# A four-layer graph network on one core: ScalarE's and VectorE's instruction orders given by the program instead of the scheduler

## The chip, the core and the metric

The kernel runs on one core of a Trainium2 chip, in one launch. The metric is the device time of that launch in microseconds (us). Five engines work side by side, each on its own list of instructions: TensorE (PE: matrix products), VectorE (DVE), ScalarE (ACT: here the exponentials), GpSimd (POOL) and SyncE (SP: it issues the transfers). An instruction waits until the work that it needs on other engines has been reported done.

## The reference

16 graphs of 1024 nodes with 128 features share one adjacency matrix (about 1 entry in 64 is set). Three layers of masked attention with 8 heads follow each other, and then a last layer in which an edge's weight depends on a sum of two node values. Cut to what matters:

```python
# layers 0, 1, 2, for every graph
Q, K, V = h @ Wq, h @ Wk, h @ Wv                        # 8 heads of 16
scores = einsum('bnhd,bmhd->bhnm', Q, K) / sqrt(16)
scores = where(adj == 0, -inf, scores)
attn = softmax(scores, axis=-1)
x = layer_norm(h + einsum('bhnm,bmhd->bnhd', attn, V) @ Wo + bo)
x = layer_norm(x + relu(x @ W1 + b1) @ W2 + b2)
# layer 3
h = x @ W;  e = leaky_relu((h @ a_src)[:, None] + (h @ a_dst)[None, :])
out = layer_norm(softmax(where(adj == 0, -inf, e)) @ h + x)
```

## The kernel before

One graph in one attention layer is a block; there are 48 of them. A block is cut into 32 steps: two groups of four heads, two halves of the queries (512 each), eight tiles `kt` of 128 keys. A step makes the scores of four heads in two pairs. Each pair fills a slot of PSUM of 128 x 1024 f32, and there are three slots, taken in turn. The masking is done in one of two ways: ScalarE takes the exponential straight from PSUM and GpSimd then multiplies by a mask of 0 and 1 (first pair, in five of eight steps), or VectorE adds a mask of 0 and a large negative number and ScalarE takes the exponential of the result (all other pairs). Whoever reads PSUM (ScalarE or VectorE) frees the slot. The numbers behind `# L` are the lines under which the profile lists an instruction.

```python
AHEAD = 4                      # a step's product with V comes four steps later
BOTH_ON_DVE = (2, 5, 7)        # kt in which VectorE masks both pairs

def slot(dtype=F32):
    return psum.tile([P, N], dtype, tag="s", name="s", bufs=3)
def bank():                    # for everything but the scores
    return psum.tile([P, 512], F32, tag="t", name="t", bufs=1)
def e_tile():
    return work.tile([P, J, 512], F32, tag="e", name="e", bufs=6)

def score_step(step):
    m, g, qh, kt = step
    e = e_tile()
    q0 = qh * 512
    for pp in range(2):
        q, k = state["Wq", g, pp], state["Wk", g, pp]
        ps = slot()
        for r in range(2):
            nc.tensor.matmul(ps[:, r * 512:(r + 1) * 512], ...)                # L395
        ev = e[:, 2 * pp:2 * pp + 2, :]
        psv = ps.rearrange("p (r q) -> p r q", q=512)
        on_pool = pp == 0 and kt not in BOTH_ON_DVE
        m = (mask01 if on_pool else mask_add)[...]
        if on_pool:
            nc.scalar.activation(ev, psv, AF.Exp, scale=HD ** -0.5)            # L402
            nc.gpsimd.tensor_mul(ev, ev, m)                                    # L403
        else:
            nc.vector.tensor_add(ev, psv, m)                                   # L405
            nc.scalar.activation(ev, ev, AF.Exp, scale=HD ** -0.5)             # L406
    return e

def av_step(step, e, acc, first, last):      # e @ V, and the sums, into the one bank acc
    ... nc.tensor.matmul(acc[...], v_bufs[...], e[:, j, :], start=first, stop=last)   # L412
def finish(g, qh, acc):                      # after eight steps
    ... with soon():
        nc.vector.transpose(tt, acc)                                           # L423
    nc.vector.reciprocal(rec, tt[:, :, HD])                                    # L425
    nc.gpsimd.tensor_mul(state["A"][...], tt[:, :, :HD], rec[...])             # L426
```

Everything else (projections of the next block, output product and feed-forward of the block before, the last layer of finished graphs) is cut into tasks. At most one task is taken up in a step, behind the step's score and V products. Its products go into the one bank `t`, which ScalarE or VectorE must empty before the next task's products can start. `soon()` raises an instruction's priority with the scheduler.

```python
# transposes (L260) -> ScalarE copy xT, x1T (L263, L265)
# split: x @ Wq, x @ Wk (L271) -> ScalarE hi (L359), VectorE lo = t - hi (L360)
# v (L271, 32 small products) -> ScalarE copy (L366)
# gather: VectorE transposes A into aT (L439), range check of the sums (L327)
# out_proj, ffn2 (L271; 32 and 64 small products) -> VectorE
def add_and_stats(n):
    def out(ts, ps):
        with soon():
            nc.vector.tensor_add(n[0][:, ts, :], v3(ps), n[0][:, ts, :])       # L303
        stats(n, ts)               # four bn_stats (L296), four bn_aggr (L298)
# then GpSimd normalises (L311 to L315)
# ffn1 (L271) -> ScalarE relu hT (L468)
# last layer: nodes (L529), edges (L569 -> VectorE L572),
#             aggregate (L581, 32 products -> VectorE L584, L587, stats)
```

The loop over all steps runs with TensorE's order fixed by the program; the orders of ScalarE, VectorE and GpSimd are chosen when the kernel is built, by a scheduler that works with priorities and its own estimate of durations. Once built, every engine's order is fixed.

```python
with tc.manual_schedule(engines={mybir.EngineType.PE}):
    for m, (b, l) in enumerate(blocks):
        ...
            e = score_step(step)
            waiting.append((step, e, n + AHEAD))
            av_due(n)              # the V products that are due, and finish()
            piece()                # one task
            n += 1
    for n in range(n, n + 2 * AHEAD):
        now[0] = n
        av_due(n)
        piece()
```

Of the kernel before, what the change touches and what calls it, by code (L numbers as in the profile page):

```python
# [14 lines left out]
AF = mybir.ActivationFunctionType  # L15
# [5 lines left out]
HD = 16  # L21
# [10 lines left out]
BOTH_ON_DVE = (2, 5, 7)  # L32
# [74 lines left out]
def fast_path(ctx: ExitStack, tc: tile.TileContext, a: dict, out: bass.AP, flag):  # L107
    nc = tc.nc
# [12 lines left out]
    def slot(dtype=F32):  # L121

        return psum.tile([P, N], dtype, tag="s", name="s", bufs=3)
# [9 lines left out]
    def e_tile():  # L133
        return work.tile([P, J, 512], F32, tag="e", name="e", bufs=6)
# [12 lines left out]
    def fetch(b):  # L147
        def run():
            state["x", b] = load_x(b)
        return run  # L150
# [60 lines left out]
    def other_weights():  # L211
        for l in range(1, L):
            W.append(load_layer(nc, nc.sync, const, a, l, [n for n in LAYER if n not in ("ln1_b", "ln2_b")]))
            norm_weights(nc.sync, l)
            add_bias(nc.sync, "ln2_b", l - 1, "bo", l)
            add_bias(nc.sync, "ln1_b", l, "b2", l)
        nc.sync.dma_start(ln2_b_last, rows_of(a[f"L{L - 1}_gnn_ln2_b"]))
        for n in LAST:
            src = a[f"L3_gnn_{n}"]
            if n == "W":  # L220
                t = w_nodes[:, :D]
                nc.sync.dma_start(t, src)
            elif n in ("a_src", "a_dst"):
                t = const.tile([P, 1], F32, name=n)
                nc.sync.dma_start(t, src.rearrange("(p o) -> p o", o=1))
            else:
                t = const.tile([P, D], F32, name=n)
                nc.sync.dma_start(t, rows_of(src))
            wl[n] = t

    def last_weights():
        a2 = const.tile([P, 2], F32)
        nc.vector.tensor_copy(a2[:, 0:1], wl["a_src"])
        nc.vector.tensor_copy(a2[:, 1:2], wl["a_dst"])
        ps = bank()
        nc.tensor.transpose(ps[:, :P], w_nodes[:, :D], identf)
        w3t = work.tile([P, P], F32, tag="row", name="w3t", bufs=2)
        nc.vector.tensor_copy(w3t, ps[:, :P])
        ps = bank()
        nc.tensor.matmul(ps[:, :2], w3t, a2, start=True, stop=True)  # L240
        nc.vector.tensor_copy(w_nodes[:, D:], ps[:, :2])
# [131 lines left out]
    def stack(m, g):  # L373

        for n, order in (("Wk", (0, 1, 0, 1)), ("Wq", (0, 0, 1, 1))):
            for pp in range(2):
                t = work.tile([P, N], F32R, tag=n, name=n, bufs=4)
                r0 = (g * J + 2 * pp) * HD
                for i, part in enumerate(order):
                    nc.sync.dma_start(t[i:P:4, :].bitcast(F32), state[n, m][part][r0:r0 + 2 * HD, :].bitcast(F32))  # L380
                state[n, g, pp] = t
# [5 lines left out]
# [8 lines that stand above are left out]
                nc.tensor.matmul(ps[:, r * 512:(r + 1) * 512], k[64 * r:64 * r + 64, kt * P:(kt + 1) * P],  # L395
                                 q[64 * r:64 * r + 64, q0:q0 + 512], start=True, stop=True)
# [3 lines that stand above are left out]
            m = (mask01 if on_pool else mask_add)[:, kt, q0:q0 + 512][:, None, :].to_broadcast([P, 2, 512])  # L400
            if on_pool:
                nc.scalar.activation(ev, psv, AF.Exp, scale=HD ** -0.5)  # L402
                nc.gpsimd.tensor_mul(ev, ev, m)  # L403
            else:
                nc.vector.tensor_add(ev, psv, m)  # L405
                nc.scalar.activation(ev, ev, AF.Exp, scale=HD ** -0.5)  # L406
        return e

    def av_step(step, e, acc, first, last):
        m, g, qh, kt = step  # L410
        for j in range(J):
            nc.tensor.matmul(acc[j * SLOT:j * SLOT + HD + 1, :], v_bufs[m % 2][:, kt, 2 * j + g, :], e[:, j, :],  # L412
                             start=first, stop=last)
# [204 lines left out]
    def put(tasks, mark, chain=None, first=False):  # L618

        if chain is None:  # L620
            chain = {"due": now[0], "queue": deque()}
            chains.insert(0 if first else len(chains), chain)
        for n, task in enumerate(tasks):
            chain["queue"].append(task + (mark if n == len(tasks) - 1 else None,))
        return chain
# [21 lines left out]
    def need(mark):  # L647
        while mark not in done:
            first = next(c for c in chains if any(q[3] == mark for q in c["queue"]))
            assert take(first) or any(take(c) for c in list(chains) if c is not first)  # L650
# [17 lines left out]
    def av_due(n):  # L668

        for item in [w for w in waiting if w[2] <= n]:  # L670
            step, e, _ = item
            half = step[:3]
            if half not in accs:
                if accs:
                    continue
                accs[half] = sums
                left[half] = NT
            waiting.remove(item)
            left[half] -= 1
            av_step(step, e, accs[half], left[half] == NT - 1, left[half] == 0)  # L680
            if left[half]:
                continue
            m, g, qh = half
            b, l = blocks[m]
            while g == 0 and qh == 0 and last_attn:
                need(last_attn.pop())
            finish(g, qh, accs.pop(half))()
            if m == len(blocks) - 1:
                if g == G - 1:
                    if qh == 0:  # L690
                        final.append(post_tasks(b, l)[1])
                    put(final[0][qh], ("final", qh), first=True)
                    if qh == 1:
                        put(last_tasks(b), ("last", b), chains[0])
            elif g == G - 1 and qh == 1:
                post = post_tasks(b, l)[0]
                chain = put(post[:1], ("attn", b, l))
                put(post[1:], ("post", b, l), chain)
                last_attn.append(("attn", b, l))
                if l == L - 1:  # L700
                    put(last_tasks(b), ("last", b), chain)

    n = 0
    with tc.manual_schedule(engines={mybir.EngineType.PE}):
        for m, (b, l) in enumerate(blocks):
            order = [(g, qh) for g in range(G) for qh in range(2)]
            if m == len(blocks) - 1:
                order.sort(key=lambda x: x[1])
            for at, (g, qh, kt) in enumerate((g, qh, kt) for g, qh in order for kt in range(NT)):
                now[0] = n  # L710
                if at == 1:
                    stack(m, 1)
                if n == 3:
                    other_weights()
                if n == 40:
                    last_weights()
                if at == 0 and m + 2 < len(blocks) and blocks[m + 2][1] == 0:
                    put([(0, fetch(blocks[m + 2][0]), "+x")], ("fetch", blocks[m + 2][0]))
                if m + 1 < len(blocks):
                    if at == 6:  # L720
                        need(("post",) + (blocks[m + 1][0], blocks[m + 1][1] - 1) if blocks[m + 1][1] else
                             ("fetch", blocks[m + 1][0]))
                        put(proj_tasks(m + 1), ("proj", m + 1), first=True)
                    if at == 19:
                        need(("proj", m + 1))
                        stack(m + 1, 0)
                step = m, g, qh, kt
                e = score_step(step)
                waiting.append((step, e, n + AHEAD))
                av_due(n)  # L730
                piece()
                n += 1
        for n in range(n, n + 2 * AHEAD):
            now[0] = n
            av_due(n)
            piece()
        while chains:
            now[0] += 1
            for chain in list(chains):
                if now[0] >= chain["due"] + chain["queue"][0][0]:  # L740
                    take(chain)
# [236 lines left out]
```

## Time and profile before

| | us |
|---|---|
| time, median of three runs (4254.99 to 4259.61) | 4256.9 |
| span of the profiled run, granted TensorE clock 0.98 | 4253.7 |
| TensorE busy | 3892.9 |
| VectorE, ScalarE, GpSimd busy | 3404.9, 3417.3, 3451.4 |
| one masking on VectorE (L405), 2112 of them | 1.212 |
| one exponential of a masked pair (L406), 2112 | 1.060 |
| one exponential from PSUM (L402), 960 | 1.021 |
| one mask product on GpSimd (L403), 960 | 2.151 |

How to read the profile: an entry such as `ACT e L406` is an engine, the tile that it writes and the line. Busy time is the union of an engine's instructions; matmuls overlap each other, and their ends are modelled. A wait is idle time ahead of an instruction, put down to whoever released it last. "PEld" is TensorE's loading of weights, which runs beside its products. In the chain that ended last, each instruction is followed back to the one that released it, and the shares of engines and lines are shares of the span.

### The profile page before, as it was taken

The numbers are of one execution on the slowest core, as the hardware profiler recorded it, in microseconds if no ns is written. First come the engines' busy times: TensorE is split into PE (matmuls) and PEld (weight loads), VectorE is DVE, ScalarE is ACT, GpSimd is POOL, SyncE is SP. The second block draws the span as 40 slices with busy tenths as digits, with TensorE's granted clock in tenths as the row PEclk, the third lists the DMA queues.
The fourth block names the chain that finished last, engine by engine and source line by source line (L and its number), as shares of the span: only waits on it lengthen the run. The fifth ranks groups of instructions, "written<-read, shape, count | busy, mean of one in ns | idle before, by whom it ended". The sixth has DMA issues, their size and how long they took to land.

```text
span 4253.7 us, 93788 instructions
## 1 busy us (share of the span) xinstructions
PE 3892.9 (92%) x37589; PEld 1575.2 (37%) x37589; DVE 3404.9 (80%) x5324; ACT 3417.3 (80%) x3961; POOL 3451.4 (81%) x3010
## 2 busy tenths in 40 slices
PE   7999999999999999999999899999999999999986
PEld 2333333344443333334444333333344433333435
DVE  6888888877777888887777888887877788888784
ACT  7999999876778898987676898997876789998770
POOL 4788888876779888888777988888877798888785
PEclk9999999999999999999999999999999999999997
DMA  5221222121211221221112212221211212212100
GB/s 147 65 61 50 52 61 61 48 63 44 51 51 48 61 61 44 57 61 51 51 44 59 59 48 55 61 61 41 56 48 49 66 41 61 60 47 55 44 24 17
DMA packets 126235, 232.23 MB, mean 55 GB/s; under 512 B 36704, under 2 KB 75616, under 8 KB 125792
## 3 DMA queue, kind: packets, MB, share of 16 engines
q1 hardware_dynamic: 122896, 225.14, 21.0%
q8 instruction: 299, 4.90, 0.5%
q10 hardware_dynamic: 2896, 1.01, 0.1%
q14 instruction: 144, 1.18, 0.1%
HBM read 15.54 MB, written 8.39 MB: 6 GB/s over the span
## 4 chain that ended last, share of the span: by engine, by line
PE 37%; DVE 26%; ACT 23%; issue 7%; POOL 5%; DMA 1%; SPq 1%; DVEq 0%; ACTq 0%; POOLq 0%
DVE e L405 16%; ACT e L406 13%; PE t L271 11%; PE acc L412 10%; PE s L395 9%; ACT e L402 6%; PE t L581 6%; DVE st L296 2%; POOL e L403 2%; DVE tt L423 1%; DVE e L572 1%; DVE x L303 1%; PE t L260 1%; ACT xT L265 1%; DVE lo L360 1%
## 5 line engine op out<-in xcount | busy, mean ns | idle before, releaser
L405 DVE TENSOR_TENSOR e<-s,mask_add 128x1024 f32<-128x1024 f32 x2112 | 2499.4, 1212 | 441.2 <-PE s L395 351.5
L406 ACT ACTIVATE e<-e 128x1024 f32<-128x1024 f32 x2112 | 2200.2, 1060 | 408.2 <-DVE e L405 392.1
L403 POOL TENSOR_TENSOR e<-e,mask 128x1024 f32<-128x1024 f32 x960 | 2054.0, 2151 | 426.1 <-ACT e L402 410.5
L412 PE MATMUL acc<-e,v 128*17 128x512 f32 x12288 | 1635.4, 604 | 56.5 <-DVE tt L423 29.8
L395 PE MATMUL s<-Wq,Wk 64*128 64x512 f32 x6144 | 1225.7, 462 | 137.9 <-ACT e L402 67.9
L402 ACT ACTIVATE e<-s 128x1024 f32<-128x1024 f32 x960 | 980.4, 1021 | 115.0 <-PE s L395 58.4
L395 PEld LDWEIGHTS s<-Wq,Wk 64*128 64x128 f32 x6144 | 505.8, 185 | 1118.5 <-issue 371.5
L412 PEld LDWEIGHTS acc<-e,v 128*17 128x17 f32 x12288 | 207.2, 95 | 558.2 <-issue 445.6
L315 POOL TENSOR_SCALAR x<-x,mv 128x128 f32<-128x128 f32 x896 | 391.4, 452 | 24.1
L319 POOL TENSOR_TENSOR x<-x,ln_g 128x1024 f32<-128x1024 f32 (+1 forms) x97 | 229.4, 2365 | 107.8 <-PE t L260 101.9
L581 PEld LDWEIGHTS t<-hd,e 128*128 128x128 f32 x2048 | 255.2, 205 | 63.7 <-issue 32.5
L581 PE MATMUL t<-hd,e 128*128 128x129 f32 x2048 | 267.2, 292 | 8.3 <-DVE x L587 3.5
L313 POOL TENSOR_TENSOR mv<-mv,half_neg 128x4 f32<-128x4 f32 x224 | 232.4, 1037 | 14.7
L271 PE MATMUL t<-x1T,W 128*32 128x512 f32 x1536 | 206.2, 609 | 18.0 <-ACT hT L468 8.6
L303 DVE TENSOR_TENSOR x<-t,x 128x512 f32<-128x512 f32 x192 | 131.8, 687 | 100.1 <-PE t L271 99.4
L296 DVE BATCH_NORM_STATS2 st<-x 128x6 f32<-128x128 f32 x896 | 196.7, 279 | 2.8
L271 PEld LDWEIGHTS t<-W,hT 128*32 128x32 f32 x6144 | 172.0, 111 | 70.6 <-issue 32.9
L271 PE MATMUL t<-W,hT 128*32 128x128 f32 x6144 | 187.1, 274 | 9.1 <-DVE x L303 5.2
L260 PE MATMUL t<-identf,x 128*128 128x128 f32 x896 | 151.5, 290 | 34.7 <-ACT xT L265 7.8
L260 PEld LDWEIGHTS t<-identf,x 128*128 128x128 f32 x896 | 95.9, 142 | 229.2 <-issue 48.0
L311 POOL TENSOR_SCALAR mv<-mv 128x4 f32<-128x4 f32 x224 | 53.0, 237 | 145.1 <-DVE mv L298 108.4
L468 ACT ACTIVATE hT<-t,b 128x512 f32<-128x512 f32 x192 | 132.3, 689 | 45.6 <-PE t L271 42.6
(83 smaller groups left out, 2509.7 us busy)
## 6 DMA issues: line engine op xcount, KB each, us to landing
Wk<-hi SPq DMA_DIRECT2D x384, 128.0 KB
Wk<-lo SPq DMA_DIRECT2D x384, 128.0 KB
Wq<-hi SPq DMA_DIRECT2D x384, 128.0 KB
Wq<-lo SPq DMA_DIRECT2D x384, 128.0 KB
x<-in_x_dram SPq DMA_DIRECT2D x16, 512.0 KB
out_dram<-x SPq DMA_DIRECT2D x31, 256.0 KB
ai<-in_adj_dram SPq DMA_DIRECT2D x8, 512.0 KB
g_rows<-parts SPq DMA_DIRECT2D x124, 4.0 KB
```

What stands on the lines that cost most here:

```text
L260: nc.tensor.transpose(ps[:, t * P:(t + 1) * P], src[:, 4 * h + t, :], identf)
L271: nc.tensor.matmul(dst[j:j + SLOT, :], lhsT[:, j:j + SLOT], rhs, start=start, stop=stop)
L296: nc.vector.bn_stats(st[:, t, :], z[:, t, :])
L313: nc.gpsimd.tensor_tensor(v, v, half_neg[:, ts], OP.pow)
L315: nc.gpsimd.tensor_scalar(z[:, t, :], z[:, t, :], mv[:, t, 0:1], mv[:, t, 1:2], op0=OP.add, op1=OP.mult)
L395: nc.tensor.matmul(ps[:, r * 512:(r + 1) * 512], k[64 * r:64 * r + 64, kt * P:(kt + 1) * P], q[64 * r:64 * r + 64, q0:q0 + 512], start=Tru ...
L402: nc.scalar.activation(ev, psv, AF.Exp, scale=HD ** -0.5)
L403: nc.gpsimd.tensor_mul(ev, ev, m)
L405: nc.vector.tensor_add(ev, psv, m)
L406: nc.scalar.activation(ev, ev, AF.Exp, scale=HD ** -0.5)
L412: nc.tensor.matmul(acc[j * SLOT:j * SLOT + HD + 1, :], v_bufs[m % 2][:, kt, 2 * j + g, :], e[:, j, :], start=first, stop=last)
L581: nc.tensor.matmul(ps[:, i * (D + 1):(i + 1) * (D + 1)], e[:, t, i * P:(i + 1) * P], s["hd"][t // 4][:, t % 4, :], start=(t == 0), stop=(t ...
```

## The change

ScalarE's and VectorE's orders in the loop are now given by the program too, as TensorE's was: each engine executes its instructions in the order in which the program writes them. So that ScalarE doesn't stand before a masking that VectorE has only just begun, the exponential of a masked pair isn't written at once but put on a list. `exponentials()` is called at the end of each step's scores and writes those that are due: the second pair's of the step before, and, in the steps in which VectorE masks both pairs, the first pair's of this one. All other work of VectorE in a step (transpose of the sums, a task's subtraction, addition and statistics) comes behind the step's maskings, as it is written there. `soon()` has no effect on these two engines any more. GpSimd's order is still the scheduler's.

```diff
@@ score_step
             else:
                 nc.vector.tensor_add(ev, psv, m)
-                nc.scalar.activation(ev, ev, AF.Exp, scale=HD ** -0.5)
+                masked.append((2 * step_no[0] + pp + (kt not in BOTH_ON_DVE), ev))
+        step_no[0] += 1
+        exponentials()
         return e
+
+    masked, step_no = [], [0]
+
+    def exponentials(n=None):
+
+        while masked and (n is not None or masked[0][0] < 2 * step_no[0] - 1):
+            _, ev = masked.pop(0)
+            nc.scalar.activation(ev, ev, AF.Exp, scale=HD ** -0.5)
@@ the loop over all steps
-    with tc.manual_schedule(engines={mybir.EngineType.PE}):
+    with tc.manual_schedule(engines={mybir.EngineType.PE, mybir.EngineType.Activation, mybir.EngineType.DVE}):
@@ after the last step
+        exponentials(0)
         for n in range(n, n + 2 * AHEAD):
             now[0] = n
             av_due(n)
```

In the changed kernel L406 is L417, and the lines from L412 on are ten or eleven higher (L412 is L422, L423 is L433).

## The prediction

> **What bounds the kernel now.** I read the page first (busy shares and the chain that ended last), then the waits, then the timeline of one block engine by engine. The page shows four engines that are all nearly full, and a chain that goes round TensorE, VectorE and ScalarE:
>
> ```profile
> PE 3892.9 (92%) x37589; PEld 1575.2 (37%) x37589; DVE 3404.9 (80%) x5324; ACT 3417.3 (80%) x3961; POOL 3451.4 (81%) x3010
> ...
> PE 37%; DVE 26%; ACT 23%; issue 7%; POOL 5%; DMA 1%; SPq 1%; DVEq 0%; ACTq 0%; POOLq 0%
> DVE e L405 16%; ACT e L406 13%; PE t L271 11%; PE acc L412 10%; PE s L395 9%; ACT e L402 6%; PE t L581 6%; DVE st L296 2%; POOL e L403 2%; DVE tt L423 1%; DVE e L572 1%; DVE x L303 1%; PE t L260 1%; ACT xT L265 1%; DVE lo L360 1%
> ```
>
> TensorE is the longest, with 4254 - 3893 = 361 us idle. No change to the other engines' orders can bring more than that plus what is hidden in stretched matmuls. The waits (engine, line, whom it waited for: us in total, times, longest) say who holds whom:
>
> ```profile
> ACT e L406 <- DVE e L405: 392.1, 446, 5.3
> DVE e L405 <- PE s L395: 351.5, 442, 7.8
> DVE col L584 <- PE t L581: 175.8, 64, 11.5
> PE s L395 <- ACT e L402: 67.9, 138, 0.9
> PE t L271 <- DVE lo L360: 41.1, 47, 1.5
> PE s L395 <- DVE e L405: 32.8, 58, 1.7
> PE acc L412 <- DVE tt L423: 29.8, 78, 0.7
> ```
>
> ScalarE's largest wait, 392 us, is for VectorE's masking; it is what the change attacks. But TensorE, the bound, loses only 68 us to a late exponential (L402, which frees a score slot), 33 us to late masking, 41 us to `lo` and 30 us to the transpose of the sums. The 392 us are mostly idle time of an engine that isn't the bottleneck.
>
> **One block in detail.** The middle of the run repeats with a period of 77.2 us for a block of 32 steps. The windows view of such a block, and of the stretch without tasks in it (us; then busy of PE, PEld, DVE, ACT, POOL; clock, DMA):
>
> ```profile
> 505.00:582.20 77.20, 72.32 (x722) 25.42 (x720) 65.30 (x97) 70.08 (x79) 67.22 (x56) 1.00 0.23 56
> 564.40:587.30 22.90, 21.25 (x148) 6.10 (x148) 22.40 (x32) 22.18 (x24) 21.50 (x21) 1.00 0.38 93
> ```
>
> From start to start of the scores in TensorE's timeline, an undelayed step costs 1.65 us without a task (572.49 to 574.14), 2.50 with eight L271 (522.51 to 525.01), 2.23 with four transposes, 2.52 with 32 and 3.39 with 64 small matmuls. A block has 14, 8, 4, 4 and 2 of these: 23.1 + 20.0 + 8.9 + 10.1 + 6.8 = 68.9 us. So a block has 77.2 - 68.9 = 8.3 us of delay, of which 77.2 - 72.3 = 4.9 show as idle and 3.4 are hidden in busy.
>
> In the stretch without tasks VectorE is 98% and ScalarE 97% busy: there it is not TensorE that sets the pace. ScalarE back to back takes 2.80 us for three exponentials (581.38 to 584.18):
>
> ```profile
> 581.38 1.02 ACT L402 ACTIVATE e<-s 128x1024 f32<-128x1024 f32 x1
> 582.28 2.01 ACT L406 ACTIVATE e<-e 128x1024 f32<-128x1024 f32 x2
> 584.18 1.03 ACT L402 ACTIVATE e<-s 128x1024 f32<-128x1024 f32 x1
> ```
>
> That is 0.93 each, 1.87 us for a step's two, above TensorE's 1.65.
>
> **What the Trainium skill says.** "PSUM — Partial Sum Buffer", section "Engine vs sequencer instructions": the queues of ScalarE and VectorE are strict first in, first out. So an order chosen by the program is binding: what stands behind a blocked instruction waits. The trace agrees (VectorE stands up to 11.5 us before L584). "ScalarE: Activation LUTs", section "What ACT_TABLE_LOAD costs": 186 ns plus 0.833 ns for each element with immediate scale and bias, and an overlap of about 93 ns back to back; for 1024 elements 1039 and 946 ns. The trace has 1021 to 1060 and 933: agreed. "VectorE: DVE Perf Modes", section "The perf-mode tier table (the rule you actually need)": an addition with a PSUM operand runs at 1x, so no order makes the 1212 ns of L405 shorter; back to back the trace has 7.95 us for seven, 1.14 each.
>
> **The change part by part.** No operation is added or taken away: 960 direct exponentials, 2112 masked ones and 2112 maskings stay. What moves is read from the two built programs' orders.
>
> 1. *ScalarE.* Before, the direct exponential of step n stood behind all masked ones of earlier steps in 683 of 960 cases, one was still owed in 230 and two in 47. After, one is owed in 959 of 960 (in steps with both maskings on VectorE the first one stays in its own step). So the direct exponential, which frees the slot, no longer waits for the last masking. I expect most of the 68 us on TensorE to go where ScalarE isn't itself full. In the ordinary block the timeline has 1.8 us of it, four times; 1.2 happen in the full stretch and stay, so the gain is some 0.6 us a block. The demand there stays: 12 steps without tasks take 562.79 to 585.78 = 23.0 us now, and ScalarE's own work is 12 x 1.87 = 22.4. The step later doesn't reduce that; it only lets ScalarE owe one, never two.
>
> 2. *VectorE, `lo`.* It now follows the step's masking at once, and no other task's work stands between. The 0.9 us that TensorE loses to it in the block (521.50, before a Wo product) goes: 0.9 gained.
>
> 3. *VectorE, statistics ahead of the next masking.* This is a loss. In steps where both maskings are on VectorE (the third, sixth and eighth of every eight), the order before was `x<-t`, first masking, statistics, second masking; the trace shows it:
>
> ```profile
> 562.93 0.69 DVE L303 TENSOR_TENSOR x<-t,x 128x512 f32<-128x512 f32 x1 [0.34 <-PE t L271]
> 563.54 1.22 DVE L405 TENSOR_TENSOR e<-s,mask_add 128x1024 f32<-128x1024 f32 x1
> 564.67 0.86 DVE L296 BATCH_NORM_STATS2 st<-x 128x6 f32<-128x128 f32 x4
> 565.45 0.36 DVE L298 BATCH_NORM_AGGREGATE mv<-st 128x2 f32<-128x6 f32 x4
> 565.73 1.19 DVE L405 TENSOR_TENSOR e<-s,mask_add 128x1024 f32<-128x1024 f32 x1
> ```
>
> After, all statistics (0.86 + 0.36, about 1.1 us with overlap) come ahead of both. The first masking frees the slot that the second score pair of the next step needs, with 0.5 to 1.4 us in hand (a step of 1.65 to 2.5 us, less some 1.15 for the masking itself). It happens twice a block (behind the first Wo product and the second W2 product): I count 1.3 and 1.0 us.
>
> 4. *VectorE, transpose of the sums.* It stood ahead of a masking at times and now always stands behind one (1.2 us) and behind the statistics before it. TensorE has one bank of sums and waits. Idle for it in the block is 0.65 + 0.16 + 0.15 now; I estimate 1.3 more in two of the four places. In blocks with tasks of the last layer both transposes of A also come later, in front of it: 1.4 us, in some 20 blocks, perhaps 20 us in all.
>
> 5. *Last layer's tasks.* Before, L584 stood ahead of maskings that were long ready. After, all of VectorE's work is in TensorE's order, so it waits only for what TensorE hasn't done. Steps with L581 take 6.2 us on average where the undelayed one takes 5.4 (64 steps), and those with L529x4 3.9 against 2.7 (16): 51 + 19 = 70 us, part of it clock (0.69 to 0.72 in some L581 windows). I expect 40 to 60 back.
>
> The sum for a block: -0.6 - 0.9 + 2.3 + 1.3 = +2.1 us, against which stands what I can't count: the 3.4 us hidden in stretched matmuls and 0.9 us of small waits for ScalarE's copies (0.26, 0.24, 0.22, 0.20), all of which come from orders that disagree with TensorE's. If half goes, -2.2: about zero, 0 x 48 blocks. With -50 from part 5, +20 from part 4, and -15 for ScalarE in the last layer's stages: 4257 - 45 = 4212, rounded to 4210 us.
>
> **Rivals.** A: the loop is cut. The 392 us of ScalarE's waiting feed back through the slots (ScalarE late, scores late, masking late), and half of the 8.3 us a block goes: 48 x 4 = 190, with part 5 4257 - 240 = 4017 us. For it: the chain's 29% in L405 and L406. Against it: only 68 us reach TensorE, and the stretch is full on two engines. B: fixed orders lose elasticity. Losses of part 3 and 4 stand, nothing hidden comes back: +2.1 x 48 = +101, less 45: 4310 us. For it: before, ScalarE could owe two in the stretch, and statistics were split. C: the masks on GpSimd (81%) become the bound; its order is still the scheduler's and changes little, 67 of 77 us a block; I give it little.
>
> **Range and chances.** The middle lies between A and B. My count of one block is uncertain by some 2 us either way, 100 us in the whole, so 8 in 10: 4100 to 4320. Under 4172 (2% faster) 0.33, over 4342 0.13, between 0.54.
>
> **What would show it.** Right: ScalarE's wait for L405 well under 200 us; TensorE's wait for L402 under 40; its wait for the transpose (acc) and for L405 up; ordinary block 76 to 78 us. Wrong: a block under 75 us means that the hidden 3.4 us were order and statistics cost nothing (A); over 79 that VectorE's fixed order is the new bound (B).

## The result and the profile after

The changed kernel takes 4360.8 us (median of four runs, 4358.65 to 4362.88) against 4255.9 for the kernel before: a ratio of 1.0245 with a 95% interval of 1.0228 to 1.0263. It is slower, where 4210 had been predicted with a range of 4100 to 4320.

The page gives the busy time of each engine in a span of 4356.9 us:

```profile
PE 3919.2 (90%) x37589; PEld 1579.8 (36%) x37589; DVE 3426.8 (79%) x5324; ACT 3385.4 (78%) x3961; POOL 3454.6 (79%) x3010
```

The instructions are the same in number. TensorE's busy time is 26 us longer and the other three stay within 1%, so most of the 103 us between the two spans is idle time of TensorE. The page's chain of the changed kernel breaks off at its last instructions and shows nothing of the loop. The waits do (engine, line, whom it waited for: us in total, times, longest):

```profile
ACT e L417 <- DVE e L405: 542.1, 355, 5.2
...
DVE lo L360 <- ACT hi L359: 151.7, 146, 2.3
...
PE s L395 <- DVE e L405: 117.3, 146, 2.3
...
PE acc L422 <- DVE tt L433: 73.2, 98, 2.2
...
PE t L271 <- DVE lo L360: 23.2, 42, 1.5
PE s L395 <- ACT e L402: 18.9, 78, 0.6
```

Of TensorE's four waits in the prediction two fell (for L402 from 67.9 to 18.9, for `lo` from 41.1 to 23.2) and two rose by more (for the masking from 32.8 to 117.3, for the transpose of the sums from 29.8 to 73.2). ScalarE's wait for the masking, which the change was to take away, rose from 392 to 542 us. VectorE now stands 152 us before `lo`, which needs ScalarE's `hi`; before, that was 44.7 us.

An ordinary block of the changed kernel, in the windows view (us; then busy of PE, PEld, DVE, ACT, POOL; clock, DMA):

```profile
589.20:667.60 78.40, 72.02 (x724) 25.26 (x720) 65.48 (x97) 69.12 (x79) 67.21 (x56) 1.00 0.21 53
```

The block is 1.2 us longer than the one shown of before, and TensorE's busy time in it is 0.3 us shorter. TensorE's timeline names its larger idle times, in brackets with whom it waited for:

```profile
600.30 0.50 PE L395 MATMUL s<-Wq,Wk 64*128 64x512 f32 x2 [1.10 <-DVE e L405]
...
613.58 1.05 PE L422 MATMUL acc<-e,v 128*17 128x512 f32 x8 [1.28 <-DVE tt L433]
...
651.37 0.50 PE L395 MATMUL s<-Wq,Wk 64*128 64x512 f32 x2 [1.03 <-DVE e L405]
...
654.35 1.05 PE L422 MATMUL acc<-e,v 128*17 128x512 f32 x8 [0.48 <-DVE tt L433]
```

VectorE's timeline at the same place shows what stands ahead of the last two:

```profile
648.33 0.69 DVE L303 TENSOR_TENSOR x<-t,x 128x512 f32<-128x512 f32 x1 [0.34 <-PE t L271]
649.06 0.87 DVE L296 BATCH_NORM_STATS2 st<-x 128x6 f32<-128x128 f32 x4
649.85 0.36 DVE L298 BATCH_NORM_AGGREGATE mv<-st 128x2 f32<-128x6 f32 x4
650.12 3.46 DVE L405 TENSOR_TENSOR e<-s,mask_add 128x1024 f32<-128x1024 f32 x3
653.49 0.71 DVE L433 STREAM_TRANSPOSE tt<-acc 128x512 f32<-128x512 f32 x1
```

The statistics, 1.1 us, pass ahead of three maskings, the first of which TensorE needs for its next slot; and the transpose that frees the bank of sums comes behind all three.

**Where the time went, by blocks.** Taken from start to start of the scores in TensorE's timeline (each block from its fifth step on, when its own V products begin; the first with the four steps ahead of it), the 48 blocks fall in two kinds. In 28 "ordinary" ones (76 to 80 us before) there is little or nothing of the last layer; in the other 20 the last layer's tasks run, or the work ends. Against before, the ordinary blocks of the changed kernel are 40.1 us longer in all and the others 57.9; some 5 us lie outside the blocks. The same count by the kind of task that a step carries, sums in us, for the kernels before and after and the first two experiments below:

| steps of the 28 ordinary blocks | before | after | e1 | e2 |
|---|---|---|---|---|
| no task (386) | 750.5 | 787.8 | 749.0 | 790.5 |
| eight L271 (220) | 613.4 | 578.8 | 563.4 | 617.4 |
| 32 or 64 L271 (164) | 500.0 | 488.5 | 490.1 | 506.2 |
| transposes L260 (117) | 279.0 | 322.9 | 312.2 | 306.0 |
| sum with the rest | 2170.5 | 2210.6 | 2141.5 | 2251.7 |

**The granted clock.** Part of the difference may come by way of TensorE's granted clock and not by waits. Over the span it is 0.980 before and 0.973 after. By the clock records of the two traces it averages 0.970 and 0.960 in the 20 other blocks, 0.998 and 0.996 in the ordinary ones. Block time times what is missing from 1 gives an estimate of the time at full clock that TensorE loses: some 20 us more in the other blocks and 5 in the ordinary ones. It is not the whole loss. In blocks 10 to 15, a stretch of the last layer, both kernels have the same mean clock, and the changed one still takes 14 us more (windows view, before and after):

```profile
815.70:1398.60 582.90, 535.34 (x5041) 235.99 (x5040) 455.22 (x748) 429.36 (x515) 454.56 (x411) 0.96 0.20 51
828.10:1425.20 597.10, 538.34 (x5043) 236.23 (x5042) 458.93 (x747) 426.81 (x515) 454.64 (x411) 0.96 0.20 50
```

The two kernels differ in order alone, so the lower clock follows from the order in some way that no run tests.

### The profile page after: what moved, and what is told of

Its sections match the earlier page's. It is cut to its first block, busy times and chain, and to the rows that moved or that the text cites. A ratio compares the mean times of both kernels' runs of the same rounds, so it can differ in the third digit from the quotient of the medians.

```text
span 4356.9 us, 93769 instructions
## 1 busy us (share of the span) xinstructions
PE 3919.2 (90%) x37589; PEld 1579.8 (36%) x37589; DVE 3426.8 (79%) x5324; ACT 3385.4 (78%) x3961; POOL 3454.6 (79%) x3010
## 5 line engine op out<-in xcount | busy, mean ns | idle before, releaser
L417 ACT ACTIVATE e<-e 128x1024 f32<-128x1024 f32 x2112 | 2200.6, 1062 | 566.1 <-DVE e L405 542.1
L422 PE MATMUL acc<-e,v 128*17 128x512 f32 x12288 | 1646.5, 608 | 103.3 <-DVE tt L433 73.2
L395 PE MATMUL s<-Wq,Wk 64*128 64x512 f32 x6144 | 1246.9, 465 | 179.7 <-DVE e L405 117.3
L402 ACT ACTIVATE e<-s 128x1024 f32<-128x1024 f32 x960 | 983.8, 1025 | 228.2 <-PE s L395 121.5
L422 PEld LDWEIGHTS acc<-e,v 128*17 128x17 f32 x12288 | 207.8, 95 | 615.0 <-issue 480.7
L319 POOL TENSOR_TENSOR x<-x,ln_g 128x1024 f32<-128x1024 f32 (+1 forms) x97 | 229.6, 2367 | 35.3 <-PE t L260 32.5
L360 DVE TENSOR_TENSOR lo<-t,hi 128x512 fp32r<-128x512 f32 x192 | 130.3, 679 | 151.7 <-ACT hi L359 151.7
L271 PE MATMUL t<-x1T,W 128*32 128x512 f32 x1536 | 201.4, 596 | 3.1 <-DVE x L597 1.0
L271 PEld LDWEIGHTS t<-W,hT 128*32 128x32 f32 x6144 | 172.2, 111 | 65.3 <-issue 27.1
L271 PE MATMUL t<-W,hT 128*32 128x128 f32 x6144 | 187.1, 274 | 2.5 <-DVE lo L360 1.1
L260 PE MATMUL t<-identf,x 128*128 128x128 f32 x896 | 152.3, 294 | 33.9 <-DVE lo L360 13.8
L260 PEld LDWEIGHTS t<-identf,x 128*128 128x128 f32 x896 | 97.5, 145 | 230.6 <-ACT xT L265 44.9
```

The lines of the kernel that those rows point to most:

```text
L260: nc.tensor.transpose(ps[:, t * P:(t + 1) * P], src[:, 4 * h + t, :], identf)
L271: nc.tensor.matmul(dst[j:j + SLOT, :], lhsT[:, j:j + SLOT], rhs, start=start, stop=stop)
L319: nc.gpsimd.tensor_mul(z, z, rows(gain, n))
```

## The experiments

V is the theory that VectorE's order, fixed as written, costs the time; S is its rival, that ScalarE's does. All kernels compute everything that the kernel before does; they differ in order alone. "Against before" is always a ratio of times measured beside each other, with its 95% interval; block sums are differences to the kernel before in us, ordinary / other, from the profiled run.

**e1: ScalarE's order fixed, VectorE's left to the scheduler.**

```diff
-manual_schedule(engines={PE, Activation, DVE})
+manual_schedule(engines={PE, Activation})
```

> The changed kernel with only ScalarE's order fixed (its exponentials a step later); VectorE is given back to the scheduler. Theory V (VectorE's fixed order costs the time: statistics, transposes of the sums and of A stand ahead of or behind maskings that TensorE waits for): the loss goes, 4200 to 4260 us, an ordinary block of 76 to 77.2 us against 77.2 before and 78.4 after. Theory S (ScalarE's fixed order costs it, as it can owe only one exponential and its copies stand behind two exponentials): 4330 to 4370 us, a block of 78 us or more.

Measured: 4239.8 us, 0.9965 of before (0.9953 to 0.9978). Blocks -29.0 / +16.9. TensorE's waits, and ScalarE's for the masking:

```profile
ACT e L417 <- DVE e L405: 377.3, 381, 6.9
...
PE s L395 <- DVE e L405: 38.4, 63, 1.7
...
PE acc L422 <- DVE tt L433: 28.9, 72, 0.7
```

V holds. With the exponentials as in the changed kernel and VectorE as before, the kernel is some 120 us faster than the changed one and a little faster than the one before. An ordinary block takes 76.1 us, where the two shown take 77.2 before and 78.4 after:

```profile
496.60:572.70 76.10, 71.63 (x726) 25.61 (x722) 65.33 (x97) 69.46 (x79) 67.01 (x56) 1.00 0.22 57
```

The table says where: steps with eight L271 gain 50 us, and the transposes give 33 of that back.

**e2: VectorE's order alone fixed** (the kernel before, no exponential delayed).

```diff
-manual_schedule(engines={PE})
+manual_schedule(engines={PE, DVE})
```

> The kernel before with only VectorE's order fixed; ScalarE stays with the scheduler, and its exponentials are not moved. Theory V: the whole loss, 4350 to 4420 us. Theory S: as before, 4240 to 4270 us.

Measured: 4405.0 us, 1.0337 (1.0300 to 1.0374). Blocks +81.2 / +63.5; TensorE's waits for the masking 108.3 us and for the transpose of the sums 78.5. VectorE's half costs more alone than the whole change does. Its cost sits in the steps without a task (+40 us in the table) and in those with transposes (+27).

**e3: all three orders fixed, exponentials at once.**

```diff
-manual_schedule(engines={PE})
+manual_schedule(engines={PE, Activation, DVE})
```

> Both orders fixed, but each masked exponential is written at once, in its own step. It tells what the delay by a step is worth when orders are fixed: if ScalarE's wait for masking matters then, over 4450 us; if it is idle time of an engine that isn't the bottleneck, within 30 us of the changed kernel's 4361.

Measured: 4752.8 us, 1.1167 (1.1149 to 1.1186). Blocks +248 / +253.

```profile
ACT e L406 <- DVE e L405: 971.1, 717, 5.8
...
DVE lo L360 <- ACT hi L359: 280.3, 177, 2.9
...
PE s L395 <- ACT e L402: 101.0, 108, 1.7
```

The delay is worth 392 us (4753 against 4361) once both orders are fixed. An exponential written at once makes ScalarE stand 971 us before maskings, and what stands behind it (L402, `hi`) reaches its readers late. So ScalarE's waiting isn't harmless in itself. In e2, where the scheduler orders ScalarE and no exponential is delayed either, the same wait is 415.5 us and the kernel 4405 us: what e3 adds comes with ScalarE's order as written.

**e4: statistics and normalisation behind the next step's maskings** (changed kernel).

```diff
-        stats(n, ts)                     # and normalise(...)
+        later.append(lambda: (stats(...), normalise(...)))
@@ step loop
+        late()            # behind av_due(n), ahead of piece()
```

> The changed kernel, both orders fixed, but a task's statistics (and the normalisation behind them) are written a step later, behind the next step's maskings and behind the transpose of the sums. Theory V: TensorE's wait for masking in steps behind Wo and W2 products (1.10 and 1.03 us a block) and two thirds of its wait for the transpose (1.28 and 0.48) go, a block of 75 to 76 us, 4220 to 4270 us. Theory S: at most 20 us less than 4361.

Measured: 4324.5 us, 1.0166 (1.0150 to 1.0183). Blocks +14.3 / +57.5. TensorE's wait for the masking falls from 117.3 to 36.3 us, its wait for the transpose from 73.2 to 62.7 only. The expectation was missed by both theories: the kernel gains some 35 us, and none of it in the other blocks. The ordinary blocks are 26 us shorter in all, which understates the edit: in eleven of them e4 is granted less than the full clock where the changed kernel has all of it. Two neighbouring blocks of e4:

```profile
426.67:503.73 77.06, 72.16 (x724) 25.31 (x721) 65.23 (x97) 69.15 (x79) 67.06 (x56) 1.00 0.23 56
503.73:581.90 78.17, 73.46 (x725) 25.46 (x722) 65.41 (x97) 69.37 (x79) 67.05 (x56) 0.98 0.23 54
```

At the full clock a block takes 77.1 us, against 78.4 in the changed kernel: the statistics ahead of the maskings cost 1.3 us of each ordinary block. The lower clock costs 1.1 us in a block that it falls in.

**e6: also the transpose of the sums ahead of that step's masking** (e4; in steps with `kt == 3` the masking is held back behind the V products and their transpose).

```diff
-                nc.vector.tensor_add(ev, psv, m)
-                masked.append(...)
+                def mask(...):       # the same two lines
+                    ...
+                if kt == 3:
+                    held.append(mask)
+                else:
+                    mask()
@@ step loop, behind av_due(n)
+                while held:
+                    held.pop(0)()
```

> As e4 (both orders fixed, statistics a step later), and in the steps that end a half of the queries VectorE's masking is written behind the transpose of the sums. If TensorE's wait for that transpose (62.7 us in e4, 69 times) is the next loss of VectorE's fixed order, it falls under 25 us, and the time to 4270 to 4300 us; if the masking that is then late costs as much, 4315 to 4340 us.

Measured: 4311.7 us, 1.0140 (1.0123 to 1.0157). Blocks -2.1 / +60.8. VectorE's timeline, at a place like the one shown of the changed kernel:

```profile
557.27 0.69 DVE L303 TENSOR_TENSOR x<-t,x 128x512 f32<-128x512 f32 x1 [0.40 <-PE t L271]
557.88 2.34 DVE L411 TENSOR_TENSOR e<-s,mask_add 128x1024 f32<-128x1024 f32 x2
560.14 0.86 DVE L296 BATCH_NORM_STATS2 st<-x 128x6 f32<-128x128 f32 x4
560.92 0.36 DVE L298 BATCH_NORM_AGGREGATE mv<-st 128x2 f32<-128x6 f32 x4
561.20 0.68 DVE L443 STREAM_TRANSPOSE tt<-acc 128x512 f32<-128x512 f32 x1
```

Two maskings now lie ahead of the statistics, and the transpose comes ahead of the third. In the waits of this kernel the transpose's falls from the 62.7 us of e4 to 15.9, as expected; most of that turns up as waiting for maskings (36.3 to 74.7):

```profile
PE s L400 <- DVE e L411: 74.7, 131, 1.6
...
PE acc L432 <- DVE tt L443: 15.9, 37, 1.1
```

Nothing comes of it in a block at the full clock, 77.0 us as in e4:

```profile
499.30:576.30 77.00, 72.77 (x726) 25.32 (x722) 65.05 (x96) 69.52 (x79) 67.08 (x56) 1.00 0.23 56
```

The ordinary blocks are 16 us shorter in all than in e4, but these are the blocks in which e4 had the lower clock and e6 has not. They are level with before and still 27 us above e1. The other blocks haven't got shorter, and the time lies between the two ranges that were named. In e6's block TensorE waits 0.4 us for the transpose instead of 1.7, but 0.6 for maskings instead of nothing, and its busy time is 0.5 us longer: what one wait gives back is taken up elsewhere.

**e7 and e8: V products three steps later instead of four, after and before.** The theory to test was that tiles of `e` run short in the last layer, whose edge task takes one of the six.

```diff
-AHEAD = 4
+AHEAD = 3
```

> The changed kernel with the product with V three steps behind the scores, not four: one tile of exponentials is free sooner. If the last layer's stages lose because ScalarE and VectorE stand before a tile that the V product of the same step must free (105 us and 56 us of waits for acc), these waits fall to a third and the blocks of 104 to 112 us get 4 us shorter at least; masks of GpSimd that come late may take it back in the other blocks.

> The kernel before with the same product three steps behind. If the shortage of tiles hurts fixed orders more than the scheduler's, this gains less than e7 does: e7's loss against this one is under 1.5%. If the loss in the last layer's stages has nothing to do with these tiles, e7 stays 2 to 3% above it.

Measured: e7 4492.5 us, 1.0566 (1.0547 to 1.0586); e8 4583.0, 1.0782 (1.0761 to 1.0803). In e7 the waits for a tile to come free are gone, but the blocks are +142 / +97.5, and blocks 10 to 15, a last-layer stretch, take 607.7 us against 597.1. A shortage of tiles isn't supported. In e8 GpSimd's mask products come too late for the sooner product: TensorE waits 206.6 us for them, against 23.8 in the kernel before. That wait drowns what was to be compared, so these two leave open why fixed orders lose less with the shorter lead.

**e10, e12, e14: the rest of e1's loss in the last layer, on ScalarE.** e10 writes the owed exponentials ahead of a direct one while an edge tile is in use; e12 puts every masked exponential a step later, also the first one where VectorE masks both pairs; e14 does both. All start from e1.

```diff
@@ e10, at the start of score_step
+        if edge_tiles[0]:
+            exponentials(2 * step_no[0] + 1)
@@ e12
-                masked.append((2 * step_no[0] + pp + (kt not in BOTH_ON_DVE), ev))
+                masked.append((2 * step_no[0] + 2, ev))
```

> As e1 (only ScalarE's order fixed), but as long as a tile of the last layer's edges is live, the owed exponentials are written ahead of the step's direct one, not behind it. If e1's loss in the last layer's blocks (110 us against 104) comes from the direct exponential that stands blocked at the head of ScalarE's queue (97.8 us of waits for acc), it goes: 4195 to 4225 us. If it comes from VectorE's order there, 4235 to 4250 us.

> As e1 (only ScalarE's order fixed), but every masked exponential comes a step later, also the first pair's in the steps in which VectorE masks both. So no exponential that needs this step's masking stands ahead of the task's copy in ScalarE's queue any more. If e1's loss in the last layer's blocks (110 us against 104) is that the one bank of the tasks is emptied late (copy behind such an exponential, then VectorE's subtraction), blocks of 104 to 107 us and 4190 to 4225 us in all; if not, 4230 to 4250 us.

> As e12, and with e10's remedy too (owed exponentials ahead of the direct one while a tile of the last layer's edges is live). If both causes act in the last layer's blocks, 15 us or more under e12; if e10's part is nothing here either, within 6 us of e12.

Measured: e10 4237.3 us, 0.9964 (0.9950 to 0.9978); e12 4253.2, 1.0010 (1.0003 to 1.0018); e14 4252.7, 1.0003 (0.9994 to 1.0011). In e10 the wait aimed at (ScalarE for a tile of `e`) falls from 97.8 to 62.8 us and the time stays that of e1. In e12 ScalarE's wait for the masking falls from 377.3 to 47.1 us, and the kernel is some 0.4% slower. Both ideas fall. With VectorE scheduled freely, 330 us of ScalarE's waiting for maskings can be taken away and nothing is gained.

**e13 and e15: the uniform delay with VectorE's order fixed**, on e6 and on the changed kernel (the edit of e12).

> As e6 (both orders fixed, statistics later, transpose of the sums first), with every masked exponential a step later as in e12. If ScalarE's copies are the rest of the loss with both orders fixed, from 4312 to 4255 us or less; if it is VectorE's fixed order itself, over 4290 us.

> The changed kernel with nothing else changed but every masked exponential a step later. If the copies behind this step's exponential cost the changed kernel its 40 to 60 us in the last layer's blocks, 4300 to 4325 us; if its loss there is VectorE's statistics and transposes, 4345 to 4365 us.

Measured: e13 4294.8 us, 1.0106 (1.0089 to 1.0123); e15 4311.6, 1.0142 (1.0125 to 1.0160). Blocks -16.4 / +56.0 and +11.3 / +44.8. In e15 ScalarE's wait for the masking falls from 542.1 to 77.9 us and VectorE's for `hi` from 151.7 to 85.1, while TensorE's two waits for VectorE stay:

```profile
PE s L395 <- DVE e L405: 110.9, 142, 1.4
...
PE acc L422 <- DVE tt L433: 81.9, 95, 2.2
```

Here the delay does pay, some 45 us against the changed kernel: 29 in ordinary blocks, 13 in the others. So the range named for e15 was hit for another reason than the one named, which put the gain in the last layer's blocks. In e13, with all remedies together, an ordinary block at the full clock takes 76.2 us, and 76.2 in e12, whose VectorE is scheduled:

```profile
1557.42:1633.66 76.24, 72.25 (x724) 24.71 (x720) 64.75 (x96) 69.34 (x80) 67.04 (x57) 1.00 0.23 58
```

In such a block nothing is left of what VectorE's fixed order costs. Of the 2.3 us by which the changed kernel's block exceeds e1's (78.4 against 76.1), the statistics account for 1.3 and the delay, on top of e6, for 0.8. In the other blocks e13 stays 31 us above e12, at a mean clock of 0.953 against 0.971.

The gain by the delay speaks for two fixed orders that lock into each other: VectorE waits in order for `hi`, `hi` stands on ScalarE behind an exponential, and that waits for VectorE's masking. In the changed kernel that is the case in the steps with both maskings on VectorE, whose first exponential isn't delayed.

**e16 and e18: the gather taken early**, on e6 and, as a control, on the kernel before. In both the transposes of A are taken in the first step in which they are due, beside that step's task. With fixed orders that moves them in the last layer's blocks alone; in the ordinary ones of e6 they already stand in that step.

```diff
+        for chain in list(chains):
+            if chain["queue"][0][1].__name__ == "both" and now[0] >= chain["due"] + chain["queue"][0][0]:
+                take(chain)
```

> As e6 (both orders fixed, statistics later, transpose of the sums first), and the gather (two transposes of A) is taken as soon as it is due, beside a step's task. If the late gather is the rest of the loss in the last layer's blocks: 4312 falls to 4275 us or less. If it isn't: 4300 to 4320 us.

> The kernel before with the gather taken as soon as it is due, as in e16: the control for the order of tasks that comes with it. Within 10 us of the kernel before if the order of tasks doesn't matter by itself; what it gains beyond that is to be taken off e16's gain.

Measured: e16 4319.1 us, 1.0166 (1.0149 to 1.0183); e18 4263.9, 1.0035 (1.0021 to 1.0049). The edit costs the kernel before 15 us, more than the 10 that were expected, and e6 7.4, so fixed orders gain some 8 us by it at most. A late gather isn't what the last layer's blocks lose by.

**e17: `lo` behind the next step's maskings** (e6).

```diff
-        nc.vector.tensor_sub(lo[:, c], ps, hi[:, c].bitcast(F32))
+        later.append(lambda: nc.vector.tensor_sub(...))
```

> As e6, and the subtraction lo comes a step later, behind the next step's maskings, so that VectorE no longer stands before ScalarE's copy. If that standing is the rest of the loss: VectorE's wait for hi falls from about 150 us to under 50, and the time to 4275 us or less. If the bank that lo frees later costs as much: 4310 us or more.

Measured: 4449.6 us, 1.0469 (1.0451 to 1.0486). Blocks +66.4 / +126.4.

```profile
PE t L271 <- DVE lo L365: 121.0, 80, 2.0
```

VectorE's wait for `hi` falls from 134.8 us (e6) to 1.9, and TensorE's wait for `lo` rises from 26.3 to 121. The bank `t` is single, so `lo` can't be late, although waiting for it in order holds up the maskings.

## Why the prediction was wrong

**ScalarE (part 1).** The gain in TensorE's wait for L402 came, 67.9 to 18.9 us ("under 40" was the mark). The reading of the 392 us as mostly idle time of no account held as long as VectorE's order was the scheduler's: e12 takes 330 us of it away and gains nothing. It didn't hold with both orders fixed: e3 puts it at 971 us and 11.7%, and e15 takes 464 us away for some 45. "Well under 200" failed, because the delay leaves the first exponential of a pair of VectorE's maskings in its own step. ScalarE's half of the change alone is a small gain (e1).

**`lo` (part 2).** Gained 0.1 us in the block instead of 0.9 (0.35 and 0.42 are left at two places), since `lo` now follows the maskings of its step, and those wait.

**Statistics (part 3).** Counted 1.3 and 1.0 us, measured 1.10 and 1.03. Moving them (e4) takes all of this wait away and returns 1.3 us of a block at the full clock: part of the wait only changes its place.

**Transpose of the sums (part 4).** Counted +1.3 us a block; measured 1.28 + 0.48 + 0.19 = 1.95 against 0.96, so +1.0. Removing that wait (e6) returned nothing in a block at the full clock, since a wait for the masking and longer busy time of TensorE took its place. The 20 us for a late gather were not found in the last layer's blocks (e16, e18); TensorE's wait for `aT` rose from 4.3 to 15.2 us, one wait of 6.2 us and 32 of about 0.3.

**The credit in the sum: the step that failed for the ordinary blocks.** The four terms, as measured, are -1.4 - 0.1 + 2.1 + 1.0 = +1.6 us, and the block became 1.2 longer: 0.4 came back at most. Against +2.1 the prediction set -2.2 for half of the time hidden in stretched matmuls and of small waits for ScalarE's copies, "all of which come from orders that disagree with TensorE's". TensorE's busy time in the block fell by 0.3, and small waits of 0.34, 0.22 and 0.27 for the copies and `aT` are still there. e1's block is 1.1 us shorter than before, and 0.9 of it is the wait for L402, which part 1 counts. So the count was nearly right; the belief that order as such gives time back was argued and not measured, and it was worth 2.2 x 48 = 106 us in the forecast. Between the forecast (-45) and the outcome of the span (+103) lie 148 us: 40 in the ordinary blocks, 103 in the others (-45 expected, +58 measured) and 5 outside.

**Last layer's tasks (part 5): the sign was wrong.** -40 to -60 was expected; the 20 other blocks are 58 us longer. The steps with the aggregate products, which I took to be 6.2 us long because VectorE's order was in the way, are 6.7 in the changed kernel, 6.8 in e1 and 6.5 in e2 (52 steps each; the prediction counted all 64 tasks, of which 12 come behind the last step). So fixing orders doesn't shorten them; fixing ScalarE's alone lengthens them. Of the 30 us that they lengthen by in e1, 20 are idle time of TensorE, before `lo` and before a score slot held by VectorE's edges (L572, here L582): 32.5 us in all against 12.7. The other 10 are busy time, at a mean clock of 0.904 against 0.926. Only the steps with four L529 got shorter as forecast, 14 steps from 54.8 to 47.2 us. The rest of the difference between e1 and the changed kernel (41 us in these blocks) is VectorE's order, spread over steps of every kind: eight L271 +11, 32 or 64 L271 +15, edges +12, no task +8. The uniform delay takes 13 off (e15). Statistics, the transpose of the sums, the gather and `lo` were each moved, and none of them brought it back. What the remaining 45 us or so against before hang on, 17 of which are in e1 as well, stays open. The granted clock is the rival that no run tests: in these blocks TensorE loses, by the estimate above, some 17 us at full clock more in e1 than before, and 34 more in e13. In the changed kernel it can't be all of it, as blocks 10 to 15 show.

**The rivals.** B, lost elasticity, named the cause in the ordinary blocks. Its 4310 still contained the gain in the last layer; without the -45, 4355 would have stood there. That this is close to the 4361 measured is luck: B counts 2.1 us in each of 48 blocks, and measured were 40 us in the 28 ordinary ones and 58 us in the others, for which B has no term. The block of 78.4 us lies between the prediction's marks for being right (76 to 78) and for B (over 79). A fell: ScalarE's wait for the masking grew, and where it went (e12) nothing was gained. C fell too: GpSimd's busy time changed by 3 us.

## What to carry to other kernels

Before fixing an engine's order by hand, ask of every instruction what waits behind it in that queue, and try one engine at a time: here ScalarE's fixed order gained 0.35% and VectorE's, with its short statistics written ahead of maskings that TensorE needed, lost 2.8% on top. An idle time that "comes from disagreeing orders" isn't a credit until an experiment has returned it. A wait between two engines that aren't the bound can be free under one order (e12) and dear under another (e3, e15), so its size alone says nothing. And before a few microseconds are put down to an edit, blocks at the same granted clock should be compared: e6 looked 16 us better than e4 in its ordinary blocks, and at equal clock the two are level.

## What the hardware showed besides

The 32 f32 products of one aggregate task take 3.84 us where the granted clock is 1.00 and 5.56 us in a window of the kernel before where it is 0.68. The steps densest in such products are thus also those whose length says least about order. VectorE's maskings take 1.21 us alone and 1.14 to 1.17 each back to back (three in 3.46, two in 2.34); ScalarE's exponentials 1.02 to 1.06 and 0.93. The overlap doesn't need a run of equal instructions: in the prediction's lines the statistics start 1.13 us after a masking that lasts 1.22. It is lost where the engine stands idle between two instructions, some 0.1 us beside the wait itself.
